# Three PSUM banks for the first image of a last layer, and another order of the SBUF pools of the layer before it

## The chip, the cores and the metric

The kernel runs on one core of a Trainium2 chip. The metric is the time of one execution on the device in microseconds (us), as the median of several runs. Everything the kernel computes, all four layers for all four images, lies in one launch.

## The reference, cut to what matters

Four images of 64 x 64 points with 128 channels pass through four layers. Each layer normalises its input over groups of four channels (`_gn`), does its own work, and adds the result to the input:

```python
x = x + _L0_conv_ref(_gn(x), ...)   # selective scan in four directions
x = x + _L1_conv_ref(_gn(x), ...)   # Fourier mixing along rows and columns, two dense layers
x = x + _L2_conv_ref(_gn(x), ...)   # attention between channels, spectral convolutions
x = x + _L3_conv_ref(_gn(x), ...)   # attention of each point to its 7 x 7 neighbours
```

The last layer, cut to its core, is this (4 heads of 32 channels, `SCALE = 32 ** -0.5`):

```python
qkv = x @ qkv_w.T + qkv_b                 # q, k, v for all points
kp, vp = pad(k, 3), pad(v, 3)             # zeros around the image
k_win, v_win = 7 x 7 windows of kp, vp
attn = softmax(einsum(q, k_win) * SCALE + bias)
out = einsum(attn, v_win) @ proj_w.T + proj_b
```

All arithmetic is in fp32.

## The kernel before, in words

The four layers run one after the other, each for all four images. The first two functions, `layer0` and `layer1`, are not touched. `layer1` (Fourier mixing) works image by image. Its last instructions for each eighth of an image are the second dense matrix (`po`, L686), a normalisation on VectorE, the addition to the input (L705) and the store to the buffer x2 in device memory (L706).

`layer2` (the third layer) takes the images in pairs. `layer2_image` is a generator that builds one image's instructions in steps. `Pace.in_turn` interleaves the generators of two images by a rough clock of its own, and `manual_schedule` keeps that order on TensorE, ScalarE, VectorE and GpSimd. The profile shows nearly all of this layer as L872, so one goes by the names of tiles. An image's input is the tile `xg`, loaded in four quarters. Its last steps scale and add up `m`, `sp` and `z`, and store `m` to the buffer x3 in four quarters. The layer makes its SBUF pools in one line: `l2big` with seven arrays of 16 KB per partition, `l2tmp` with work tiles, and `l2small` with columns.

`layer3` (the last layer) first makes a pool of weights and of padded key images, `l3w`. It loads six weight arrays (L1412), clears a tile `zero` on VectorE (L1418), clears the edges of the key images `kp` on GpSimd (L1421), and clears the edges of two padded value images `v_pads` in device memory by eight transfers from `zero` (L1423, L1425). Then it makes its working pools and, under `manual_schedule`, does the following:

- `front(b)` loads image b (`x3`, in four quarters) and then has four parts. The norm: for each of eight chunks of 512 points, four transposes into a PSUM tile `pg` (L1443), `bn_stats` on VectorE (L1444), and a copy to `xn` on ScalarE (L1445). The scale and offset of the groups (L67 to L79) and their application (L1451). The values: for each chunk four products into a PSUM tile `pv` (L1456), the bias added into an SBUF tile `vt` on VectorE (L1464), and two stores to `v_pads` (L1467). The keys: for each chunk one product into a PSUM tile `pk` (L1471), and an ScalarE instruction that puts it into `kp` (L1474).
- `queries(b, by)` computes the queries of a row of eight blocks (`pq`, L1485, `q`, L1489) and loads the 16 value windows `V` of that row (L1500).
- The loop runs over 128 units of two blocks each, as a software pipeline: scores `ps` (L1561), bias and maximum (L1572, L1579), exponentials (L1552), the division on GpSimd (L1545), transposes `pt` (L1507), the product with the values `po` (L1595).

For image 0, `front(0)` and `queries(0, 0)` run in full before the loop. For images 1 to 3 the pieces of `front` are dealt out one by one between the units of the image before.

In PSUM the layer has three kinds of pools that matter here. `psM` has one bank, and `pg`, `gn_gm`, `gn_gv`, `pv`, `pk`, `pq` and `pj` all share it through one tag. `psS` has two buffers of two banks for the scores `ps`. `psT` and `psO` hold the transposes and the products with the values. Before the loop starts, `psS` is not in use.

All stores and loads named above are issued by SyncE, whose queue is executed in order: a transfer that has to wait holds up those behind it. SyncE's place for each transfer is set by the scheduler when the program is built.

SBUF pools are laid out in order of creation. A pool that is made after others have been closed may get their bytes. In the built program the first instructions on such a pool wait for the last users of every closed pool whose bytes it overlaps, whichever of the pool's tiles they touch. In the kernel before, the bytes of each partition are these:

| pool | bytes |
|---|---|
| layer1: `l1big` (input images and others) | from 32096 |
| layer2: `l2big` | 32096 to 146784 |
| layer2: `l2tmp`, `l2small` | 146784 to 228224 |
| layer3: `l3w` (weights, `kp`, `zero`) | 32096 to 77568 |
| layer3: `l3big` (`x3`, `xn`) | 77568 to 143104 |

So `l2big` takes bytes of `l1big`, and `l3w` takes bytes of `l2big`.

Of the kernel before, what the change touches and what calls it, by code (L numbers as in the profile page):

```python
# [2 lines left out]

# [7 lines left out]
F32 = mybir.dt.float32  # L11
# [5 lines left out]
P = 128  # L17
# [5 lines left out]
CH = 512  # L23
# [685 lines left out]
def load_image(nc, x, x_dram):  # L709
    for q in range(4):  # L710
        nc.sync.dma_start(
            x[:, 8 * q : 8 * q + 8, :], x_dram[1024 * q : 1024 * q + 1024, :].rearrange("(j p) d -> p j d", p=P)
        )
# [652 lines left out]
def layer2(sh, w, wp, x_in, x_out, scr, wt):  # L1366
    tc, nc = sh.tc, sh.nc
    with ExitStack() as ctx:
        pool = lambda name, bufs, **kw: ctx.enter_context(tc.tile_pool(name=name, bufs=bufs, **kw))
        ps = pool("l2ps", 3, space=PSUM)  # L1370
        for name, shape in (("XG", [64, 5, P]), ("BD", [P, P])):
            w[name] = [wp.tile(shape, F32, name=f"{name}{n}") for n in range(2)]
            for t in w[name]:
                nc.vector.memset(t, 0.0)
        for t in w["XG"]:
            nc.vector.memset(t[:, 4, 64:65], 1.0)
        pools = pool("l2big", 1), pool("l2tmp", 1), pool("l2small", 1), ps
        paced = copy(sh)
        paced.nc = Pace(nc)
        engines = {mybir.EngineType.PE, mybir.EngineType.Activation, mybir.EngineType.DVE, mybir.EngineType.Pool}  # L1380
        free = [0, 1]
        pairs = [[] for _ in range(NB // 2)]

        def image(b):
            n = free.pop(0)
            yield from layer2_image(paced, w, pools, x_in(b), x_out(b), (scr(n), scr(2 + n)), wt, n, pairs[b // 2])
            free.append(n)

        with tc.manual_schedule(engines=engines):
            paced.nc.in_turn((image(b) for b in range(NB)), 2)  # L1390


def layer3(sh, A, x_in, out, v_pads):
# [5 lines left out]
    with ExitStack() as ctx:  # L1399
        pool = lambda name, bufs, **kw: ctx.enter_context(tc.tile_pool(name=name, bufs=bufs, **kw))  # L1400
# [25 lines left out]
        big, tmp, small = pool("l3big", 2), pool("l3tmp", 2), pool("l3small", 4)  # L1426
        psS, psT = pool("l3psS", 2, space=PSUM), pool("l3psT", 2, space=PSUM)
        psO, psM = pool("l3psO", 1, space=PSUM), pool("l3psM", 1, space=PSUM)
# [2 lines left out]

        def front(b):

            x = big.tile([P, NJ, DM], F32, name="x3")
            load_image(nc, x, x_in(b))
            xn = big.tile([P, NT], F32, name="xn3")
            image[b] = x, xn
            yield
            st = small.tile([P, NCH, 6], F32, name="gn_st", bufs=2)
            for c in range(NCH):  # L1440
                pg = psM.tile([P, CH], F32, name="pg3", tag="m")
                for q in range(4):
                    nc.tensor.transpose(pg[:, q * P : (q + 1) * P], x[:, 4 * c + q, :], sh.ident)  # L1443
                nc.vector.bn_stats(st[:, c, :], pg)  # L1444
                nc.scalar.copy(xn[:, c * CH : (c + 1) * CH], pg)  # L1445
                yield
            s_, o_ = sh.group_scale(st, psM, small, "m")
            yield
            for c in range(0, NT, NT // 2):
                xc = xn[:, c : c + NT // 2]  # L1450
                nc.vector.tensor_scalar(xc, xc, s_, o_, ALU.mult, ALU.add)  # L1451
            yield
            for c in range(NCH):
                pv = psM.tile([P, 4, P], F32, name="pv3", tag="m")
                for q in range(4):
                    nc.tensor.matmul(  # L1456
                        pv[:, q, :],
                        lhsT=xn[:, (4 * c + q) * P : (4 * c + q + 1) * P],
                        rhs=w["qkv"][:, 2 * P : 3 * P],
                        start=True,  # L1460
                        stop=True,
                    )
                vt = tmp.tile([P, 4, P], F32, name="vt")
                tt(vt, pv, w["v_b"].unsqueeze(1).to_broadcast([P, 4, P]), ALU.add)  # L1464
                rows = v_pads[b % 2][3 + 8 * c : 11 + 8 * c, 3:67, :].rearrange("(q r) c d -> r c q d", r=2)
                for r in range(2):
                    nc.sync.dma_start(rows[r], vt[64 * r : 64 * r + 64])  # L1467
                yield
            for c in range(NCH):
                pk = psM.tile([P, CH], F32, name="pk3", tag="m")  # L1470
                nc.tensor.matmul(  # L1471
                    pk, lhsT=w["qkv"][:, P : 2 * P], rhs=xn[:, c * CH : (c + 1) * CH], start=True, stop=True
                )
                nc.scalar.activation(  # L1474
                    kps[b % 2][:, 3 + 8 * c : 11 + 8 * c, 3:67],
                    pk.rearrange("p (h w) -> p h w", w=64),
                    AF.Identity,
                    bias=w["qkv_b"][:, 1:2],
                )
                yield  # L1480
# [49 lines left out]
        with tc.manual_schedule(engines=engines):  # L1530
            for _ in front(0):
                pass
            rows = {0: queries(0, 0)}
            for s in range(NU + 6):
                b, p = divmod(s, 32)
# [18 lines left out]
                if s < NU:  # L1554
                    q, V = rows[s // 4]
                    ps = psS.tile([P, 2, CH], F32, name="ps3")
# [52 lines left out]
                if p == 7 and b + 1 < NB and s < NU:  # L1609
                    pieces = front(b + 1)  # L1610
# [12 lines left out]
def network(tc, A, out):  # L1623
    nc = tc.nc
    with ExitStack() as ctx:
        const = ctx.enter_context(tc.tile_pool(name="const", bufs=1))
        dram = ctx.enter_context(tc.tile_pool(name="dram", bufs=1, space=bass.MemoryType.DRAM))
        sh = Shared(tc, const, A)
        x1, x2, x3 = ([dram.tile([NT, DM], F32, name=f"x{n}_{b}") for b in range(NB)] for n in (1, 2, 3))
        scr = [dram.tile([NT, DM], F32, name=f"scr{n}") for n in range(4)]  # L1630
        wt = dram.tile([32, 2, 8 * Q], F32, name="wt2")
        l0 = {n: dram.tile([NT, 2 * P], F32, name=f"l0_{n}") for n in ("y0", "y1", "y20", "y21", "y3")}
        l0 |= {n: dram.tile([2, P, NT], F32, name=f"l0_{n}") for n in ("xr0", "xr1", "xw0", "xw1", "z0", "z1", "z2")}
        l0 |= {f"W{n}": dram.tile([4, WD], F32, name=f"l0_W{n}") for n in ("00", "01", "10", "11")}
        l0 |= {f"B{n}": dram.tile([NS, CH], F32, name=f"l0_B{n}") for n in range(3)}
        layer0(sh, A, lambda b: A["x"][b], lambda b: x1[b], l0.__getitem__)
        l2w = ctx.enter_context(tc.tile_pool(name="l2w", bufs=1))
        w2 = layer1(sh, A, lambda b: x1[b], lambda b: x2[b], l2w, wt)
        layer2(sh, w2, l2w, lambda b: x2[b], lambda b: x3[b], lambda n: scr[n], wt)
        v_pads = [dram.tile([70, 70, DM], F32, name=f"l3_v{n}") for n in range(2)]  # L1640
        layer3(sh, A, lambda b: x3[b], lambda b: out[b], v_pads)
# [182 lines left out]
```

## Time and profile before

| | |
|---|---|
| median of 3 runs | 8356.34 us (8350.67 to 8357.69) |
| span of the profiled execution | 8355.5 us |
| busy: TensorE, VectorE, ScalarE, GpSimd | 79%, 81%, 76%, 66% |

The answer of the trace for four stretches of time, one for each layer, gives this (busy us of each engine, and the share of full speed that TensorE's clock was granted):

| layer | stretch, us | length | TensorE | VectorE | ScalarE | clock |
|---|---|---|---|---|---|---|
| 0 | 0 to 6071 | 6071.0 | 4802.08 | 5452.26 | 5453.76 | 0.97 |
| 1 | 6071 to 6690 | 619.0 | 518.34 | 307.94 | 152.92 | 0.91 |
| 2 | 6690 to 7743 | 1053.0 | 761.45 | 564.87 | 340.35 | 0.81 |
| 3 | 7743 to 8355.5 | 612.5 | 510.23 | 431.58 | 386.01 | 0.90 |

How to read it: the shares of the whole span are those of layer 0, which takes nearly three quarters of the time and is not touched. What the change concerns lies in the joints between the layers 1, 2 and 3, and in the first 85 us of the last layer. There the chain of waits has to be read piece by piece in order of time. Its rows give a start, a length, and the engine with the tile and line, or `SPq` for the issue of a transfer by SyncE, or `DMA` for a transfer's way from issue to landing.

### The profile page before, as it was taken

Reading aid. Unit: us, or ns where it says so; the run is one execution under the profiler, and the core shown is the slowest. Engines: PE = TensorE matmul, PEld = TensorE weight load, DVE = VectorE, ACT = ScalarE, POOL = GpSimd, SP = SyncE. Lnnn points to the kernel's source line nnn. Section 1 sums busy time; section 2 is a strip of 40 time slices with the busy share of each in tenths; the row PEclk is TensorE's granted clock in tenths of the full one; section 3 lists DMA queues with packets and bytes.
Section 4 is the critical chain, followed back from the end, with each engine's and each line's share of the span. In section 5 each row is a group of like instructions: output and inputs, shape, how many; then the busy total and the mean of one; then the engine's idle time right before and its main releaser. Section 6 shows DMA issues by size and latency. Waiting matters only on the chain.

```text
span 8355.5 us, 140584 instructions
## 1 busy us (share of the span) xinstructions
PE 6592.1 (79%) x52976; PEld 4182.2 (50%) x52976; DVE 6756.6 (81%) x7952; ACT 6333.0 (76%) x10320; POOL 5485.2 (66%) x2502
## 2 busy tenths in 40 slices
PE   7588888778788777888887777787778978686689
PEld 3344454444445444444544444454457756464456
DVE  2689999998899999889999999999944545645578
ACT  6799999999899889989989999999822213315467
POOL 0689889988888889888888999999800011020233
PEclk9799999999999999999999999999989988788799
DMA  6445555444555554455555445554432041331332
GB/s 111 132 144 179 166 170 173 164 160 156 169 169 177 175 171 153 154 176 159 175 173 175 163 153 181 177 175 169 165 94 52 18 118 38 86 100 31 95 93 78
DMA packets 1281978, 1163.79 MB, mean 139 GB/s; under 512 B 637973, under 2 KB 1075825, under 8 KB 1214354
## 3 DMA queue, kind: packets, MB, share of 16 engines
q1 hardware_dynamic: 1279618, 1153.06, 43.6%
q8 instruction: 417, 6.83, 0.3%
q14 instruction: 263, 2.15, 0.1%
q10 hardware_dynamic: 1680, 1.74, 0.1%
HBM read 962.66 MB, written 189.74 MB: 138 GB/s over the span
## 4 chain that ended last, share of the span: by engine, by line
PE 21%; ACT 11%; DVE 10%; issue 3%; POOL 2%; DMA 2%; SPq 1%; ACTq 0%; DVEq 0%; POOLq 0%
DVE h L484 4%; ACT hT L381 4%; ACT dA L483 4%; PE pt L371 2%; POOL dB L477 1%; PE po L686 1%; PE pf L681 1%; PE pz L872 1%; PE pt L1507 1%; PE pu L872 1%; DVE in_st L872 1%; PE pb L872 1%; PE ps L1561 1%; DVE m L872 1%; PE pa L872 1%
## 5 line engine op out<-in xcount | busy, mean ns | idle before, releaser
L484 DVE TENSOR_TENSOR_SCAN h<-dA,state,dB 128x512 f32<-128x512 f32 x4096 | 4962.0, 1270 | 379.5 <-ACT dA L483 269.8
L477 POOL TENSOR_TENSOR dB<-du,Bb 128x1024 f32<-128x1024 f32 x2048 | 4820.0, 2385 | 567.4 <-DVE h L484 398.0
L371 PE MATMUL pt<-ident,h 128*128 128x128 f32 x16384 | 2256.9, 282 | 1023.1 <-ACT hT L381 1018.9
L371 PEld LDWEIGHTS pt<-ident,h 128*128 128x128 f32 x16384 | 1846.3, 143 | 2063.8 <-ACT hT L381 1815.1
L483 ACT ACTIVATE dA<-delta,A_neg 128x512 f32<-128x512 f32 x4096 | 2745.6, 690 | 157.8 <-DVE h L484 136.7
L381 ACT COPY hT<-pt 128x1024 f32<-128x1024 f32 x2048 | 2068.9, 1010 | 182.5 <-PE pt L371 169.3
L406 PE MATMUL yT<-hT,W 128*32 128x256 f32 x16384 | 1400.9, 415 | 2.7 <-DVE y L422 2.1
L872 POOL COPY XG<-Xs 64x9 f32<-64x9 f32 (+2 forms) x44 | 11.0, 294 | 1024.9 <-ACT Xs L872 1024.9
L406 PEld LDWEIGHTS yT<-hT,W 128*32 128x32 f32 x16384 | 454.3, 150 | 353.6 <-issue 338.4
L206 PE MATMUL cv<-xn,taps 128*128 128x512 f32 x1152 | 620.1, 639 | 8.7 <-DVE e L222 8.7
L1545 POOL TENSOR_TENSOR S<-S,sm 128x784 f32<-128x784 f32 x128 | 191.4, 1495 | 408.2 <-DVE sm L1543 347.3
L317 PE MATMUL dp<-xd,w_dt 65*128 65x512 f32 x512 | 300.0, 669 | 105.4 <-ACT Ct L304 92.0
L326 POOL TENSOR_TENSOR du<-delta,u 128x1024 f32<-128x1024 f32 x128 | 305.1, 2384 | 78.5 <-DVE delta L323 78.5
L206 PEld LDWEIGHTS cv<-xn,taps 128*128 128x128 f32 x1152 | 185.5, 190 | 248.5 <-issue 244.6
L298 PE MATMUL xd_ps<-u,w_x 128*48 128x512 f32 x512 | 251.1, 614 | 44.0 <-DMA u<-l_xw 19.8
L1552 ACT ACTIVATE S<-S,mx 128x196 f32<-128x196 f32 x512 | 227.9, 448 | 32.7 <-DVE mx L1579 32.2
L682 ACT ACTIVATE h<-pf,b 128x512 f32<-128x512 f32 x128 | 88.0, 687 | 145.0 <-PE pf L681 145.0
L323 DVE SCALAR_TENSOR_TENSOR delta<-delta,dp 128x512 f32<-128x512 f32 x256 | 169.3, 661 | 27.7 <-ACT delta L321 27.7
L317 PEld LDWEIGHTS dp<-xd,w_dt 65*128 65x128 f32 x512 | 79.4, 195 | 220.7 <-ACT Ct L304 150.6
L1421 POOL MEMSET kp<- 128x210 f32 (+1 forms) x8 | 1.8, 287 | 275.0 <-DMA x<-m 275.0
L320 ACT ACTIVATE delta<-dp 128x512 f32<-128x512 f32 x256 | 152.4, 595 | 30.1 <-PE dp L317 25.6
L1507 PE MATMUL pt<-ident,S 128*98 128x128 f32 x1024 | 165.2, 285 | 4.4 <-POOL S L1545 1.9
(336 smaller groups left out, 7282.4 us busy)
## 6 DMA issues: line engine op xcount, KB each, us to landing
Bb<-l_B SPq DMA_DIRECT2D x512, 1024.0 KB
W<-l_W SPq DMA_DIRECT2D x512, 256.0 KB
l_y<-y SPq DMA_DIRECT2D x128, 512.0 KB
u<-l_xw SPq DMA_DIRECT2D x64, 512.0 KB
y<-l_y SPq DMA_DIRECT2D x64, 512.0 KB
u<-l_xr SPq DMA_DIRECT2D x64, 512.0 KB
V<-l_v SPq DMA_DIRECT2D x512, 49.0 KB
wr<-wt SPq DMA_DIRECT2D x128, 136.0 KB
```

What stands on the lines that cost most here:

```text
L206: nc.tensor.matmul(pm, lhsT=taps[:, s, t, :], rhs=xn[:, dy : dy + 8, dx : dx + 64], start=(t == 0), stop=(t == 8),)
L298: nc.tensor.matmul(xd_ps, lhsT=w_x[:, s, k, :], rhs=u[:, s, :], start=(s == 0), stop=(s == 1))
L317: nc.tensor.matmul(dp, lhsT=w_dt[:, k, s * P : (s + 1) * P], rhs=xd, start=True, stop=True)
L326: nc.gpsimd.tensor_tensor(du, delta, u, ALU.mult)
L371: nc.tensor.transpose(pt[:, j, s, :], G["h"][:, s, t0 : t0 + 32, :].rearrange("p t n -> p (t n)"), sh.ident)
L381: return lambda: nc.scalar.copy(hT, pt.rearrange("p j s d -> p j (s d)"))
L406: nc.tensor.matmul(U["yT"][e][32 * jo : 32 * jo + 32, qo % 2, :], lhsT=U["Ws"][G["g"]][:, :, 4 * q + j], rhs=hT[:, j, :], start=((e, jo) n ...
L477: nc.gpsimd.tensor_tensor(dB, du, B_now[:, q : q + 1, :].to_broadcast([P, 2, CH]), ALU.mult)
L483: nc.scalar.activation(dA, delta[:, s, :], AF.Exp, scale=A_neg[:, k, s, n : n + 1])
L484: nc.vector.tensor_tensor_scan(h[:, s, :, q], dA, dB[:, s, :], state[:, s, n : n + 1], ALU.mult, ALU.add)
L872: r = f(*args, **kw)
L1507: nc.tensor.transpose(pt[:, half, hp, :], U["S"][:, e, hp, 98 * half : 98 * half + 98], sh.ident)
```

## The change

The change has two parts. In `front`, a counter gives the PSUM tiles of image 0 in turn to three banks: one of three goes to `psM` as before, and two of three take the first half of a buffer of `psS`. For the images 1 to 3, and for `gn_gm`, `gn_gv`, `pq` and `pj`, nothing changes. In `layer2` the pools are made in another order, with `l2big` last.

```diff
@@ layer2
-        pools = pool("l2big", 1), pool("l2tmp", 1), pool("l2small", 1), ps
+        tmp, small, big = pool("l2tmp", 1), pool("l2small", 1), pool("l2big", 1)
+        pools = big, tmp, small, ps
@@ layer3, front
+            ring = itertools.count()
+
+            def bank(name):
+                if b == 0 and next(ring) % 3:
+                    return psS.tile([P, 2, CH], F32, name="ps3")[:, 0, :]
+                return psM.tile([P, CH], F32, name=name, tag="m")
+
...
-                pg = psM.tile([P, CH], F32, name="pg3", tag="m")
+                pg = bank("pg3")
...
-                pv = psM.tile([P, 4, P], F32, name="pv3", tag="m")
+                pv = bank("pv3").rearrange("p (q d) -> p q d", q=4)
...
-                pk = psM.tile([P, CH], F32, name="pk3", tag="m")
+                pk = bank("pk3")
```

The first part is meant to let TensorE fill one bank while VectorE and ScalarE empty another. The second part moves the bytes: `l2tmp` then lies at 32096 to 99424, `l2small` behind it, and `l2big` at 113536 to 228224. The pool of weights of the last layer, at 32096 to 77568 as before, then overlaps `l2tmp` and no longer `l2big`, and `l2big` no longer overlaps `l1big`.

On TensorE, ScalarE, VectorE and GpSimd the order of the instructions of the layers stays as it was, but for the clearing of `zero` and the scaling of the query bias on VectorE and the clearing of edges on GpSimd, which now stand in the tail of the third layer. On SyncE the transfers move as follows. The eight loads of `xg` for the first pair of images stand directly behind the last store of layer 1, ahead of all `wr` loads; four of those stood ahead of them before. The 14 transfers of weights and zeros (L1412, L1423, L1425) stand in the tail of the third layer, before the stores of its last images, where they wait for the last products `pb` of that layer. The loads of `x3` follow directly on the last store of the third layer.

More of the change, by code (lines that the diff above doesn't have):

```diff
@@ L1 @@
+import itertools
 from contextlib import ExitStack
```

## The prediction

> **What bounds the kernel now.** I read the table of stretches first, to see which layers have slack, and then the chain of waits in order of time at the two joints and in the first part of the last layer. There it runs through every instruction of image 0, one behind the other. Columns: start, length, what.
>
> ```profile
> 6690.04 2.98 DMA x<-x
> 6693.02 0.02 SPq L872
> 6693.04 0.03 issue
> 6693.07 4.46 DMA xg<-x
> 6697.53 0.45 issue
> 6697.98 3.66 PE pg L872 x16
> ```
>
> The third layer's input is loaded only when layer 1's last store has landed. The same happens at the next joint, with 14 issues of SyncE after the landing (shown in part):
>
> ```profile
> 7739.86 3.17 DMA x<-m
> 7743.11 0.35 SPq L1412
> ...
> 7749.98 0.61 SPq L1425
> 7750.59 0.04 issue
> 7750.63 4.42 DMA x<-x
> ...
> 7755.29 1.10 PE pg L1443 x4
> 7756.48 0.71 DVE gn_st L1444
> 7757.26 0.59 ACT xn L1445
> 7757.86 0.04 issue
> 7757.90 1.13 PE pg L1443 x4
> ...
> 7782.55 2.09 PE pv L1456 x8
> 7784.66 0.70 DVE vt L1464
> 7785.37 0.04 issue
> 7785.41 2.09 PE pv L1456 x8
> ```
>
> With one bank, chunk n+1 starts when chunk n has been emptied: 2.6 us a chunk in the norm, 2.86 us in values and keys. The table of stretches (length, busy us of TensorE, its weight loads, VectorE, ScalarE, GpSimd, then the clock) shows what this does to the clock:
>
> ```profile
> 6698.00:6702.00 4.00, 4.00 (x21) 3.97 (x22) 2.43 (x4) 0.00 (x0) 0.00 (x0) 0.55 1.16 291
> 6702.00:6704.20 2.20, 1.61 (x13) 1.17 (x11) 2.01 (x4) 0.00 (x0) 0.00 (x0) 1.00 1.17 290
> 7780.00:7828.00 48.00, 34.98 (x82) 18.46 (x81) 6.37 (x9) 6.00 (x9) 0.00 (x0) 0.50 0.30 82
> ```
>
> 73% busy keeps half clock for 48 us; dense transposes reach full clock within 4 us.
>
> **What the Trainium skill says.** "TensorE: Matmul & The Clock Gate", Part 1: the clock stands at half by default and is released after about 3.4 us of sustained work. The trace agrees: work starts at 6697.98 and the mean of 0.55 over 4 us puts the release near 6701.6, 3.6 us later. "PSUM — Partial Sum Buffer", PSUM bank collisions: two engines must not touch one bank at once, two reads included; so inside a chunk the copy on ScalarE stays behind `bn_stats`, as the rows at 7756.48 and 7757.26 show, and only other banks give overlap. "DMA: Bandwidth & Descriptors", Anatomy of one DMA: a fixed part of about 2 us, mostly until the last byte is confirmed. The trace has 2.42 us for a store of `vt` (chain, 7918.13), and that is what I use.
>
> **The change part by part.**
>
> *Joint of layers 1 and 2.* The last store is issued at 6690.04 and takes SyncE 0.50 us. The first load of `xg` now stands behind it in the queue and waits for products and ScalarE work done by 6686.5. So it is issued at 6690.6 instead of 6693.07: 2.5 us. I keep 4.46 us to landing. Bounds 2.0 (the store's bytes are still in the engines) and 3.0 (four `wr` loads no longer ahead). All later work of the layer hangs on this chain in the same order, so all shifts. The `wr` loads are needed 200 us later.
>
> *Joint of layers 2 and 3.* The load of `x3` overlaps bytes of the third layer and still waits for its last store, which lands at 7743.03. The 14 issues between (7743.11 to 7750.59) are gone from here: 7.5 us. Bounds 7.3 and 8.0, the latter if the load lands sooner with no zero stores in flight. What the 14 cost where they now stand: SyncE reaches them at 7674.4, when the last `pb` is done, needs some 7.5 us, and in the run before had nothing to issue from 7671.71 to 7689.33. Behind them wait the stores of `m` and the reloads of `sp`, first due at 7689.33. VectorE's clearing of `zero` (0.38 us) falls into a gap of 1.83 us before 7679.35, in which VectorE waits for `in_pm`. The scaling of the bias (0.15 us) waits for its load; with 1.75 us from issue to use as before, that is there by 7677, and VectorE reaches the place near 7682. GpSimd (1.81 us of clearing) idles there for 275 us. So 0 to 0.3 us; I take 0.
>
> *Norm of image 0.* From the first transposes to `gn_gm` it takes 7755.29 to 7775.57 = 20.3 us. With three banks a chunk can follow each 0.86 us at half clock (four transposes at 0.213). A bank comes back after 1.10 + 0.09 + 0.70 + 0.08 + 0.59 = 2.6 us, a third of which is 0.87. A quarter of the image (two chunks) lands each 1.5 us (512 KB at 346 GB/s). So the last chunk starts near 6.1 us, at full clock or nearly, and ends at 6.7; `bn_stats` and aggregation take it to 7.9, `gn_gm` to 8.3. Saved: 12.0 (11.5 to 12.5). The chain from `gn_gm` to the first `pv` (4.15 us) stays; in it TensorE does nearly nothing and falls back to half clock, as it did by 6708.3.
>
> *Values.* Before: 8 x 2.86 = 22.9 us. Now PSUM is no longer the limit, but `vt` has two tiles, so group c waits until the stores of group c-2 have landed. A store takes SyncE 0.61 (median), two 1.24; landing 2.42 later; between the pairs the queue has two loads of `V` at 0.73. From the first `pv` (0): `vt` 0 is done at 2.8 and 1 at 4.6 (TensorE, 1.78 a group at half clock). Stores of 0 land at 6.6, so `vt` 2 ends at 7.3; stores of 1 land at 8.4, so 3 ends at 9.1. SyncE then issues in order, with landings at 11.9 and 13.2 (`vt` 4 at 12.6, 5 at 13.9), 16.4 and 17.7 (6 at 17.1, 7 at 18.4). This is a wait the row of `vt` hardly shows before, 1.1 us in one instance (front of image 1).
>
> *Keys and queries.* Key group 0 needs the bank of `vt` 5, 1 that of 6, 2 that of 7. From group 1 (17.1) TensorE is dense: half clock, 1.75 a group, until about 20.8, then 0.9 (a key product took 1.06 at full clock in the loop, with its tail). Group 7 ends at 25.4, `pq` at 26.4, `q` at 27.1, the first `ps` at 27.3. Before, first `pv` to first `ps` was 7779.72 to 7828.40 = 48.7. Saved: 21.4. At half clock throughout, the first `ps` is at 32.1: 16.5.
>
> *The loop.* It then runs as before. The ten remaining `V` loads of the first row follow the last `vt` stores: near 19.7 + 10 x 0.73 = 27, while the first `po` comes 12.6 us after the first `ps`.
>
> Sum: 2.5 + 7.5 + 12.0 + 21.4 = 43.4. 8356.3 - 43.4 = 8313.
>
> **The rivals.**
>
> 1. *TensorE stays at half clock in values and keys.* For: it did so for 48 us at 73% busy, and stores of `vt` leave gaps again. Against: from key group 1 nothing interrupts it. 43.4 - 4.9 = 38.5: 8318.
> 2. *The `vt` stores don't bind.* For: one wait of 1.1 us was all in the loop. Against: there the groups come 3.5 us apart. Two groups at half clock, 14 at 0.9, `pq` and `q`: first `ps` at about 18.5, saved 30: 8304.
> 3. *The loop doesn't take the gain of the values and keys*, because the `V` loads, some 48 for three rows, now start later relative to the loop and hold it. Against: row 1 is needed some 25 us after the first `ps` and done 11 us after it. It would leave 22: 8334.
> 4. *Not faster.* The third layer is 1053 us long at a mean clock of 0.81, in which TensorE is busy 761. If its shift of 2.5 us against the windows of the clock lowered the grant to 0.77, TensorE would take some 5% longer; were all of that on the chain, some 45 us are lost: about 8358, slower than before. For: the clock there swings between 0.5 and 1. Against: order and gaps of the layer stay the same, so hits and misses should even out.
>
> **How the numbers follow.** Forecast 0.56, rival 1 0.20, rival 2 0.12, rival 3 0.07, rival 4 0.05. The range 8300 to 8330 holds the forecast and the first two rivals with the bounds of the joints (1 us) and of the run medians (the three runs before span 7 us), and leaves out rivals 3 and 4. Rivals 1 to 3 are all over 0.2% (17 us) faster: 0.95. Of rival 4 I give 0.03 to no difference and 0.02 to slower.
>
> **What would show it.** In the profile of the changed kernel: `xg` issued about 0.5 us after the last store of layer 1; no L1412 between the last `x<-m` and the load of `x3`; first `pg` to `gn_gm` in 8 to 9 us; `vt` released by DMA from its third group on; the clock at 1.0 in the last key groups; first `pv` to first `ps` in 27 us; the stretch from there to the end as long as before (527 us). The prediction is wrong if the third layer's stretch changes its length by over 5 us, if VectorE stalls near its tail for `qkv_b`, or if the loop waits for `V`.

## The result

| | before | after |
|---|---|---|
| median of 4 runs | 8353.5 us (8348.6 to 8357.7) | 8318.2 us (8312.7 to 8325.7) |
| span of the profiled execution | 8355.5 us | 8311.1 us |
| mean clock of TensorE | 0.942 | 0.948 |

After over before is 0.9959, with a 95% interval from 0.9941 to 0.9976: faster, by about 34 us. The forecast was 8313, with a range from 8300 to 8330. The two profiled executions differ by 44.4 us and the medians by 35.3; the runs of the changed kernel spread over 13 us. Its profiled execution is one of two short ones (8312.9 and 8312.7; the other two took 8323.6 and 8325.7), and that of the kernel before one of its longer ones (8356.3), so the profiles show more of a gain than the medians.

### The profile page after: what moved, and what is told of

It reads as the page before. It is cut to its first block, busy times and chain, and to the rows that moved or that the text cites. A ratio compares the mean times of both kernels' runs of the same rounds, so it can differ in the third digit from the quotient of the medians.

```text
span 8311.1 us, 140578 instructions
## 1 busy us (share of the span) xinstructions
PE 6570.4 (79%) x52976; PEld 4173.6 (50%) x52976; DVE 6756.3 (81%) x7952; ACT 6330.8 (76%) x10320; POOL 5482.4 (66%) x2502
## 4 chain that ended last, share of the span: by engine, by line
PE 21%; DVE 11%; ACT 10%; issue 3%; POOL 2%; DMA 2%; SPq 1%; ACTq 0%; DVEq 0%; POOLq 0%
DVE h L485 5%; ACT hT L382 4%; ACT dA L484 3%; PE pt L372 2%; POOL dB L478 1%; PE po L687 1%; PE pf L682 1%; PE pt L1516 1%; PE pz L873 1%; PE pu L873 1%; DVE in_st L873 1%; PE pb L873 1%; PE ps L1570 1%; PE pa L873 1%; DVE m L873 1%
## 5 line engine op out<-in xcount | busy, mean ns | idle before, releaser
L873 POOL COPY XG<-Xs 64x9 f32<-64x9 f32 (+2 forms) x44 | 10.9, 292 | 1027.8 <-ACT Xs L873 1027.8
L1561 ACT ACTIVATE S<-S,mx 128x196 f32<-128x196 f32 x512 | 227.9, 448 | 34.1 <-DVE mx L1588 33.5
L322 ACT ACTIVATE delta<-delta 128x512 f32<-128x512 f32 x256 | 162.4, 634 | 7.9
```

The costliest lines, as they stand in the source:

```text
L873: r = f(*args, **kw)
```

## The profile after

The chain of waits at the joint of layers 1 and 2 (start, length, what):

```profile
6689.73 0.36 SPq L707
...
6690.19 0.45 SPq L873
...
6692.40 7.35 DMA xg<-x
6699.75 0.14 issue
6699.88 0.64 PE pg L873 x4
```

The first `xg` load is issued 0.46 us after layer 1's last store, where it was 3.03 before. The wait for the store's landing is gone from the chain, and what holds the first norm now is the landing of the load's last quarter.

The chain at the joint of layers 2 and 3, and through the norm of image 0:

```profile
7740.31 3.17 DMA x<-m
7743.49 0.02 issue
...
7743.69 3.78 DMA x<-x
7747.47 0.24 issue
7747.71 1.09 PE pg L1452 x4
7748.80 1.71 PE ps L1452 x8
7750.51 0.94 PE pg L1452 x4
7751.45 0.87 PE ps L1452 x4
...
7755.14 0.38 DVE gn_mv L68
...
7755.66 0.37 PE gn_gm L70 x2
```

The 14 issues are gone from between the last store and the load of `x3`. From the last store's issue to the first `pg` it takes 7.40 us (15.43 before). The transposes follow one another through three banks (two of them bear the name `ps`), and `gn_gm` comes 7.95 us after the first `pg` (20.28 before).

The chain through the values:

```profile
7759.42 2.07 PE ps L1465 x8
7761.49 1.64 PE pv L1465 x8
...
7763.15 0.70 DVE vt L1473
...
7763.87 0.57 SPq L1476
...
7764.49 2.38 DMA l_v<-vt
...
7767.00 0.70 DVE vt L1473
```

The last row is the fourth `vt`: it waits until the second store of the second one, issued at 7764.49, has landed 2.38 us later (the third waits in the same way for the first). VectorE's waits in this stretch (us in total, times, longest) say it of all six groups from the third on:

```profile
DVE vt L1473 <- DMA l_v<-vt: 9.4, 6, 3.7
```

The table of stretches (columns as in the table before) shows what the clock does with these gaps:

```profile
7764.00:7768.00 4.00, 3.21 (x27) 2.83 (x26) 1.38 (x2) 0.00 (x0) 0.00 (x0) 1.00 0.47 120
7768.00:7772.00 4.00, 0.90 (x8) 0.71 (x7) 0.65 (x1) 0.00 (x0) 0.00 (x0) 1.00 0.57 147
7772.00:7776.00 4.00, 3.12 (x11) 1.55 (x11) 1.35 (x3) 0.69 (x1) 0.00 (x0) 0.64 0.57 149
7776.00:7780.00 4.00, 4.00 (x5) 1.67 (x6) 0.77 (x2) 1.00 (x2) 0.00 (x0) 0.50 0.53 138
7780.00:7784.00 4.00, 4.00 (x10) 1.71 (x9) 0.00 (x0) 3.12 (x5) 0.00 (x0) 1.00 0.28 77
```

TensorE reaches full clock, idles at the `vt` wait (0.90 us busy in 4), does the first keys at half clock, and the last at full clock. From the first `pv` to the first `ps` it takes 26.48 us (48.68 before).

**One link of this chain misleads.** Further on, the chain runs through SyncE's issues of `V` loads and then ends them like this:

```profile
7788.58 2.42 DMA V<-l_v
7791.00 0.03 issue
7791.03 1.50 POOL S L1554
```

That reads as if GpSimd's first division waited for a `V` load. But `S` is divided by `sm`, whose reciprocal on VectorE ran from 7790.77 to 7790.95. Experiment e3_vt8 tells which of the two it was.

## Where the first joint's gain went

The last `x<-m` is issued at 7740.31, and it was at 7739.86 before: although layer 2's first group scale (`gn_s`) comes 3.2 us earlier, the layer ends 0.45 us later. TensorE's products in the two traces, put side by side by their place in its order, are 2.2 to 4.0 us ahead until 7107, and 3.8 us there. There the chain of waits has this, before:

```profile
7111.34 1.99 PE pa L872 x8
7113.34 1.93 PE pb L872 x8
7115.26 1.09 PE pu L872 x8
```

and after:

```profile
7107.52 3.78 PE pa L873 x8
7111.31 3.46 PE pb L873 x8
7114.76 1.09 PE pu L873 x8
```

The same 16 products start 3.82 us earlier and end 0.50 us earlier: 1.79 + 1.53 = 3.32 us are lost in them. There is no wait between them. The stretch in which most of them run has the clock (the third number from the end) at 1.00 before and at 0.50 after:

```profile
7112.00:7116.00 4.00, 4.00 (x22) 2.35 (x21) 0.04 (x1) 2.10 (x5) 0.00 (x0) 1.00 0.00 0
```

```profile
7108.00:7112.00 4.00, 4.00 (x10) 2.57 (x11) 0.00 (x0) 1.61 (x3) 0.00 (x0) 0.50 0.00 0
```

The Trainium skill, "TensorE: Matmul & The Clock Gate", Part 1, says that the clock follows a free-running window of activity, so that the same kernel meets full clock at different instructions from run to run. That fits; what these runs show is only that the same products got another clock. This is the largest single change of the lead and not the only one: it grows again to 2.8 us near 7340, turns to 0.8 us behind at 7470, and ends 0.3 to 0.5 us behind.

## The experiments

The stages of all runs from their profiles, in us. "1>2": from layer 1's last store to layer 2's first `gn_s`. "2": from there to the last `in_d` of layer 2 that is made from `in_st`; TensorE's 5468 products in it are the same in all runs. "2>3": from that `in_d` to `gn_gm` of the last layer. "3": `gn_gm` to first `ps`. "Loop": from there to the end. The last columns give the median of the runs, and the ratio of the runs to those of the kernel before on the same chip, with its interval (it is not the quotient of the two medians); a single run has no interval.

| run | 1>2 | 2 | 2>3 | 3 | loop | median | ratio |
|---|---|---|---|---|---|---|---|
| before | 17.2 | 1013.7 | 54.7 | 52.8 | 527.1 | 8353.5 | |
| after | 14.3 | 1017.3 | 34.4 | 30.2 | 525.2 | 8318.2 | 0.9959 [0.9941, 0.9976] |
| e6_after | 14.5 | 1016.3 | 34.4 | 31.2 | 526.2 | 8312.9 | 0.9952 [0.9938, 0.9966] |
| e1_pools | 14.6 | 1018.0 | 47.0 | 52.8 | 524.0 | 8351.5 | 0.9989 [0.9981, 0.9997] |
| e2_banks | 17.6 | 1024.1 | 42.0 | 29.7 | 526.7 | 8327.5 | 0.9960 [0.9947, 0.9972] |
| e4_norm | 14.3 | 1014.8 | 34.1 | 52.3 | 528.0 | 8339.1 | one run |
| e5_two | 14.6 | 1019.2 | 37.3 | 29.6 | 523.9 | 8317.3 | 0.9953 [0.9941, 0.9966] |
| e3_vt8 | 15.0 | 1021.3 | 34.3 | 22.4 | 520.0 | 8309.2 | 0.9938 [0.9925, 0.9950] |
| e7_vt4 | 14.2 | 1013.4 | 34.5 | 22.8 | 518.6 | 8297.9 | one run |
| e11_onebank_vt8 | 17.5 | 1018.5 | 54.5 | 52.9 | 521.9 | 8361.0 | one run |
| e12_before | 17.1 | 1013.4 | 54.7 | 52.8 | 527.0 | 8358.5 | one run |
| e8_early | 14.5 | 1017.1 | 29.5 | 22.0 | 521.1 | 8298.2 | 0.9924 [0.9910, 0.9938] |
| e9_stats | 14.6 | 1016.5 | 23.8 | 21.9 | 517.3 | 8288.9 | 0.9921 [0.9907, 0.9934] |
| e10_warm | 14.6 | 1020.4 | 23.9 | 19.7 | 521.9 | 8289.1 | 0.9923 [0.9911, 0.9936] |

Columns 2>3 and 3 move only when something in them is changed, and else repeat to 1.6 us. Column 2 moves by up to 10.7 us between kernels that do the same work there. The kernel before measured 8363.5 beside e1, e2, e3 and e8, 8359.0 beside e5, e6, e9 and e10, and 8362.4 (one run) beside the four single runs; so ratios are to be compared, not medians.

**e1_pools: the order of the pools alone.**

```diff
-        pools = pool("l2big", 1), pool("l2tmp", 1), pool("l2small", 1), ps
+        tmp, small, big = pool("l2tmp", 1), pool("l2small", 1), pool("l2big", 1)
+        pools = big, tmp, small, ps
```

> The order of the pools alone, one bank as before. My theory: the two joints are shorter by 2.9 us (xg loads right behind the last store) and 8.0 us (from the last store's issue to the first pg 7.4 us where it was 15.4), and the first 85 us of the last layer stay: first pg to gn_gm 20.3, first pv to first ps 48.7. So 8353.5 - 8.0 - 2.9 = 8342.6, if layer 2 keeps what its joint gives it. Rival, the clock: what a joint ahead of layer 2 gives or takes is lost or doubled inside the layer by where half-clock stretches of TensorE fall, so that only the 8.0 is sure: 8339 to 8349. Rival, no effect of the pools (the 14 issues cost as much in the tail as they did at the joint): 8353.

Measured: joint 1>2 shorter by 2.6 us, 2>3 by 7.7 (54.7 to 47.0), the rest of the front unchanged. The median is 8351.5 beside 8363.5. The theory's stages hold, and the rival of no effect falls. That of the clock stays open: column 2 is 4.3 us longer in this profile than in that of the kernel before. The 14 transfers cost nothing in the tail: from the last `in_d` to the last store it takes 19.01 us in this run, in before and in after.

**e2_banks: the three banks alone**, with the old line for the pools.

> The three banks alone, pools in the old order. My theory: the parts are independent, so first pg to gn_gm is 8.0 us (20.3 before), first pv to first ps 26.5 (48.7 before), the joints stay as before (15.4 us from the last store's issue to the first pg): 8353.5 - 12.3 - 22.2 = 8319, or 8317 if the loop is again 2 us shorter. Rival: the two parts need each other (the zero stores, still in flight beside the first vt stores, make these later): first pv to first ps 29 or more, 8322 or above.

2>3 is shorter by 12.7 us, 3 by 23.1, and the first `pv` to the first `ps` takes 26.1 us: the parts are independent, and the rival falls by its stage. The time of 8319 was missed (8327.5), but it was worked out from 8353.5; beside 8363.5 the gain is 36 us where 34.5 were expected. The stages that it shares with the kernel before (columns 1>2 and 2) are together 10.8 us longer, which hides a third of the gain in this profile. The ratio of the runs (0.9960) equals that of the whole change: its interval, 10 us to each side, doesn't resolve the pools' part there.

**e4_norm: three banks for the norm, one for values and keys.**

```diff
-                pv = bank("pv3").rearrange("p (q d) -> p q d", q=4)
+                pv = psM.tile([P, 4, P], F32, name="pv3", tag="m")
...
-                pk = bank("pk3")
+                pk = psM.tile([P, CH], F32, name="pk3", tag="m")
```

> The change with three banks for the norm alone, values and keys on one bank as before. My theory: the parts of the sum are separate: first pg to gn_gm 7.9 us as in the change, gn_gm to the first ps 52.8 as before, so 22.6 us longer than the change from the last store to the end. Rival, the stretches share a cause (the clock: a norm at full clock leaves TensorE faster in the values): gn_gm to first ps under 50.

First `pg` to `gn_gm` takes 7.7 us, `gn_gm` to the first `ps` 52.3: as the theory said, and the rival (under 50) falls. From the last store to the end it is 595.4 us, 24.6 more than the first profile of the change and 22.6 more than the second.

**e5_two: psM every second time.**

```diff
-                if b == 0 and next(ring) % 3:
+                if b == 0 and next(ring) % 2:
```

> Every second PSUM tile of image 0 on psM instead of every third, so psM comes round after two chunks. My theory: a bank's round of 2.6 us sets the norm's pitch, 1.3 us a chunk with two and 0.87 with three: first pg to gn_gm 11.4 us (7.9 in the change); values and keys are held by the landings of the vt stores and keep their 30.2 us from gn_gm to the first ps: 3.5 us longer than the change in all. Rival, two banks are enough (VectorE or the load sets the pitch of the norm): no difference to the change. Rival, PSUM also holds values and keys: gn_gm to first ps 33 or more.

First `pg` to `gn_gm` is 10.9 us (7.9 in the change), 3 stays at 29.6. The bank's round sets the pitch of the norm, as the chain shows: two chunks for each round of `pg`, `gn_st`, `xn`, 2.53 us apart:

```profile
7753.81 1.13 PE pg L1452 x4
...
7754.97 0.71 DVE gn_st L1453
...
7755.70 0.59 ACT xn L1454
...
7756.34 1.13 PE pg L1452 x4
```

The third bank is worth 2.9 us in the norm, and nothing in values and keys.

**e3_vt8 and e7_vt4: more tiles for `vt`** (eight, as shown, and four).

```diff
-                vt = tmp.tile([P, 4, P], F32, name="vt")
+                vt = tmp.tile([P, 4, P], F32, name="vt", bufs=8)
```

> The change with eight vt tiles instead of two. My theory (the landings of the vt stores hold values and keys): no vt waits for a DMA; two groups at half clock, the others at 0.9 to 1.0, first pv to first ps near 18.5 us (26.5 in the change), the rest as long as before: 8318 - 8 = 8310, loop unchanged because the first row's V loads end near 25 us after the first pv and the first po comes at 30. Rival: TensorE's half clock holds the stretch, first pv to first ps 24 or more: 8316. Rival: issues of SyncE hold the start of the loop, as the chain of the changed kernel says (SPq, then V): then the first po stays where it was, some 38.7 us after the first pv, and the time is 8318.

> The change with four vt tiles. My theory, from the landings of the run with eight (the pair of stores of group k lands near 6.1 + 1.55 k us after the first pv): only group 7 still waits, by 0.5 us: gn_gm to first ps 22.9 (22.4 with eight, 30.2 with two). Rival: a wait for one landing holds the next stores too, and it runs away as with two tiles: 26 or more.

With eight tiles 3 takes 22.4 us and with four 22.8 (two: 30.2 and 31.2), and the first `pv` to the first `ps` 18.8 us with eight (18.5 expected). VectorE's waits for `vt` name only TensorE with eight:

```profile
DVE vt L1473 <- PE ps L1465: 2.8, 5, 1.0
DVE vt L1473 <- PE pv L1465: 1.4, 3, 1.0
```

With four there is a rest, in three groups rather than the one expected, and most of it costs nothing:

```profile
DVE vt L1473 <- DMA l_v<-vt: 2.7, 3, 2.0
```

So the landings of the `vt` stores were the bound, as the prediction had it, and two of its rivals fall: the clock alone doesn't hold the stretch, and the stores do bind. The chain's hint at SyncE falls too. With eight tiles no `V` load is issued before 7781.24 (in the change the first stood at 7765.35, between the stores), yet the loop starts 1 us earlier, and the chain enters it without SyncE:

```profile
7784.81 0.94 PE ps L1570 x16
...
7789.70 0.19 DVE sm L1552
7789.89 0.07 issue
7789.95 1.50 POOL S L1554
```

First `ps` to first `pt` is 6.69 us in both runs, although in this one the sixteenth `V` load is issued near 7793 (24 issues took 19.30 us from 7781.24 on), after that division has ended. GpSimd's wait is for `sm`; the `V` landing in the chain of the changed kernel was a coincidence of 0.05 us.

More `vt` tiles also shorten the loop, which was expected unchanged. The values of images 1 to 3 are made in its first three quarters: from the maximum (`mx`) of the first unit to that of the 97th it takes 411.7 to 415.7 us in the eight runs with two tiles, and 405.7 to 410.3 in the six with four or eight. How the tiles do this isn't shown: in the loop of the changed kernel VectorE waits for a landing of `vt` once, for 1.4 us.

**e11_onebank_vt8: the kernel before, with eight `vt` tiles.**

> The kernel before, with eight vt tiles. My theory: with one bank a group takes 2.86 us, longer than two tiles need, so nothing is gained in the first image: gn_gm to first ps 52.8 as before; in the loop, where the values of images 1 to 3 wait for landings here and there, some 4.5 us are gained as in the other runs with eight tiles: 8349. Rival: vt was a limit beside the bank already: gn_gm to first ps 50 or less.

3 stays at 52.9, and the loop is 5.1 us shorter. So bank and `vt` limit one behind the other: only when the banks are there do the tiles matter in the first image. The time of 8349 was missed (8361.0): column 2 was 4.8 us longer than in the first profile of before, which took back the loop's gain, and the two layers ahead of it were together 4.0 us longer (layer 1 some 7 longer, layer 0 some 3 shorter).

**e6_after: the changed kernel again; e12_before: the kernel before again.**

> The changed kernel itself again, as the measure for its neighbours. My theory: the last layer repeats to 1 us (last store to gn_gm 15.3, gn_gm to first ps 30.2), while the layers before it, whose instructions are the same, differ by up to 10 us from the profile of the first run, because the grant of TensorE's clock falls on other instructions each time. Rival, the layers before repeat as well, and the spread between runs has its place in the last layer, at the vt stores: then gn_gm to first ps differs by several us.

> The kernel before again, for the length of layer 2, whose instructions are the same in all runs with the old order of the pools. My theory: from the last store of layer 1 to the last store of layer 2 took 1049.8 us in the first profile and 1060.6 in that of the three banks alone; a third value will fall anywhere between 1047 and 1062, by where TensorE runs at half clock. Rival: the three banks, or the chip, made the 1060.6: 1049 to 1051.

Of e6 the last layer repeats to 2.0 us (1 was expected), and the layers before it came within 2.0 us as well, so its profile decides between neither theory. Its five runs reach from 8308.0 to 8322.6, a spread like that of the first four (8312.7 to 8325.7). e12 came out at 1049.5 us from store to store, inside the rival's range, so it decides nothing by itself; but e11, whose layer 2 is the same work without the three banks, took 1055.0 on the same chip. Banks and chip are thereby not needed for a difference of 5 us.

Over all 14 profiles column 2 goes from 1013.4 to 1024.1. But the two pairs of profiles of one kernel lie close: 1013.7 and 1013.4 before, 1017.3 and 1016.3 after. So no two runs of one kernel show the 10 us; they lie between kernels, and on several chips. In the layers ahead, where all kernels issue the same products, one kernel does differ from itself: from before to e12 the way to layer 1's first `pu` is 5.6 us shorter and the way from there to its last store 7.3 us longer. Whether chance, the chip or something fixed in each kernel sets column 2 stays open.

**e8_early, e9_stats, e10_warm: beyond the change.** The load of `x3` for image 0 waits for bytes only; its data have been in memory since the second pair of images began. e8 (with eight `vt` tiles) therefore places `l3big` first, on the bytes of `l2tmp`, with a small pool for `zero` and the query bias behind it, and `l3w` after these:

```diff
+        big, zp = pool("l3big", 2), pool("l3z", 1)
+        first = big.tile([P, NJ, DM], F32, name="x3")
+        load_image(nc, first, x_in(0))
...
         wp = pool("l3w", 1)
```

> Eight vt tiles, and the pool of the last layer's images placed first, on the bytes of the third layer's work tiles, with zero and the query bias behind it; the weights then wait for the third layer's end. My theory (the load of x3 waits for the bytes, not for its data, which have been in memory since the second image pair began): x3 is loaded near 7683, in the tail of the third layer, the first pg stands ready before the last store, and the norm begins when VectorE is done with the third layer, near the issue of the last store: some 7 us less between it and gn_gm plus 1 to 2 us of overlap of the norm's start, so 8310 - 8.5 = 8301.5. The five weight loads (some 3 us of issue after the last store has landed) are there before the first pv. Rival: the weights or the key edges, which now wait for the third layer's last store, take the place of x3: then the first pv comes no earlier than about 7743.5 + 5 + 2.4 and some 3 us are gained: 8307. Rival: loads and zero stores in the tail hold up the last stores of m: joint as before, 8310.

`x3` is loaded from 7671.08 on, 66 us ahead of the last store, and its first three chunks are transposed 13 us before it. But 2>3 falls by 4.8 us against e3, not by 8.5; the medians, 8309.2 and 8298.2, differ by 11.0, so the time alone would have passed for a confirmation. VectorE's timeline (start, length, engine, line, operation; in brackets the idle time before, and what ended it) has the reason:

```profile
7740.05 0.70 DVE L1458 BATCH_NORM_STATS2 gn_st<-pg 128x6 f32<-128x512 f32 x1 [3.39 <-DMA x<-m]
```

The first `bn_stats` waits for the last store's landing, by a rival that I hadn't named: not the weights, but the tile of the statistics, whose pool lies on the stored tile's bytes. e9 gives that tile another place:

```diff
+        st0 = zp.tile([P, NCH, 6], F32, name="gn_st0")
...
-            st = small.tile([P, NCH, 6], F32, name="gn_st", bufs=2)
+            st = small.tile([P, NCH, 6], F32, name="gn_st", bufs=2) if b else st0
```

> The version with the early load of x3, with the statistics of image 0 (gn_st) also on bytes of the third layer's work tiles. There the first bn_stats began 3.37 us after the last store's issue, at its landing. My theory: that wait was for the bytes of gn_st, which lie on those of the last stored tile; now bn_stats follows VectorE's last m directly: last store to gn_gm 7.1 us instead of 10.45, so 3.4 us less. Rival: the copies to xn, or something else that waits for the landing (the weights' pool), take its place: 10.4 as before.

2>3 falls by another 5.7 us to 23.8; 3.4 were expected. VectorE's order has changed with it: `bn_stats` now stands between the last instructions of layer 2, ahead of the store:

```profile
7735.48 1.23 DVE L873 TENSOR_TENSOR m<-m,sp 128x1024 f32<-128x1024 f32 x1
7736.62 0.69 DVE L1459 BATCH_NORM_STATS2 gn_st<-pg 128x6 f32<-128x512 f32 x1
7737.23 1.21 DVE L873 TENSOR_TENSOR m<-m,z 128x1024 f32<-128x1024 f32 x1
7738.36 1.29 DVE L1459 BATCH_NORM_STATS2 gn_st<-ps 128x6 f32<-128x512 f32 x2
```

The last store is 1.0 us later by this, and `gn_gm` follows its issue by 3.7 us (7.1 expected, 15.3 in the change). At 0.9921 against 0.9952 beside it, e9 is the shortest version: 8288.9 us, 24 less than the change on the same chip.

e10 adds to e9 six groups of transposes into idle banks, around the group statistics; the results aren't read:

```diff
+            warm(2)
             s_, o_ = sh.group_scale(st, psM, small, "m")
+            warm(4)
```

> The same with six groups of four transposes into the idle banks of psT around the group statistics, whose results nobody reads: two before gn_gm, four after gn_gv; nothing else is changed. My theory: TensorE falls to half clock because it idles for 4 us between the last pg and the first pv; kept at work, it begins the values at full clock, and two to three groups take 0.9 us instead of 1.7 to 2.1: gn_gm to first ps 22.0 before, 19.5 here. Rival: the transposes don't fill the wait well enough (VectorE's steps between leave 1 us gaps), or a part of them ends after xn is ready: gn_gm to first ps 22 or more.

3 falls from 21.9 to 19.7 us, as expected. The stretch in which the values begin, at 7746.23 in e9 and at 7748.74 in e10, behind the last of the added transposes:

```profile
7746.00:7750.00 4.00, 3.77 (x17) 3.77 (x18) 2.12 (x3) 0.00 (x0) 0.00 (x0) 0.50 0.02 4
```

```profile
7746.00:7750.00 4.00, 3.43 (x29) 3.19 (x30) 3.11 (x6) 0.26 (x1) 0.36 (x2) 1.00 0.49 129
```

The first eight products of the values take 2.08 us in e9 and 1.16 in e10. But the reason that was expected is not right: in e9 the idle chain doesn't drop the clock, which is at 0.50 ahead of it already, as it is in e10:

```profile
7738.00:7742.00 4.00, 2.22 (x8) 1.42 (x8) 3.21 (x6) 2.15 (x4) 0.16 (x1) 0.50 0.45 131
```

```profile
7738.00:7742.00 4.00, 3.43 (x15) 2.63 (x13) 3.96 (x6) 1.18 (x3) 0.00 (x0) 0.50 0.43 129
```

The added transposes bring the clock up before the values begin. In the whole time it doesn't show (0.9923 beside 0.9921): column 2 and the loop of its profile are 8.5 us longer than e9's.

## Why the prediction was right

By its steps, with what the first profile of after has for each:

| step | forecast | measured |
|---|---|---|
| joint of layers 1 and 2 | 2.5 | 2.9 at `gn_s`; -0.8 (a loss) at the last store of layer 2 |
| joint of layers 2 and 3 | 7.5 | 8.0 |
| the 14 transfers in the tail | 0 to 0.3 | 0 |
| norm of image 0 | 12.0 | 12.3 |
| `gn_gm` to first `pv` | 0 | 0.4 |
| values, keys, queries | 21.4 | 22.2 |
| loop | 0 | 1.9 |

- **First joint.** The size was right at its place; the sentence that all later work shifts with it was not. In these two profiles it shifts as far as the first products that get another clock. Rival 4 named this mechanism and bounded it at 45 us (its 5% of the 761 us of TensorE is nearer 40); column 2 differs by 10.7 us over 14 profiles. Whether some of the 2.9 us remains on average can't be told from this spread: with the new order column 2 has 1013.4 to 1021.3, with the old one 1013.4 to 1024.1, and the mean is 1017.4 in both. The sign of a wrong prediction, a change of layer 2 by over 5 us, is thereby within what the layer differs by without the change: from before to e2, 10.4 us.
- **Second joint.** The upper bound came true, as was said with it, because the first quarter of `x3` landed sooner, in 3.78 us rather than 4.42. From its issue to the first `pg` it takes 4.0 to 4.3 us in all runs that load it there with the new order and 4.5 to 4.7 in those with the old one; that it is the zero stores that were in the way isn't shown by itself.
- **Norm.** Right in size and cause; e5 shows the cause, the round of a bank.
- **Values and keys.** Right in cause: the landings of `vt` hold six groups, and e3, e7 and e11 show that they, not the bank, were what remained. From the first `pv`, the last `vt` ends at 18.0 us (forecast 18.4), TensorE reaches full clock in the keys near 20.6 (20.8), and the first `ps` comes at 26.5 (27.3). Not foreseen was the full clock in between, from 7764 to 7772.
- **Loop.** Unchanged within its spread: from the first `ps` to the end, the runs with two `vt` tiles have 523.9 to 528.0 us.
- **The sum** of 43.4 us compares with 44.4 in the two profiles and 46.1 between the medians of e6 and its before; the first medians had 35.3. That it comes so near the profiles is in part luck: instead of the 2.5 us of the first joint there are -0.8 at the end of layer 2, and the loop's 1.9 us and small gains in the other steps make up for them. The median of 8318.2 is just the time of rival 1, so the time alone could not have told that rival from the forecast; the profile does.

Rival 1 (half clock throughout values and keys) and rival 2 (no `vt` wait) are both refuted by the rows above; rival 3 (the loop waits for `V`) by the time from first `ps` to first `po`, 12.24 us (12.62 before), and by the loop, which is no longer than before.

## What to carry to other kernels

When a single PSUM bank is the limit, ask what becomes the limit with three: here it was the number of SBUF tiles whose stores must land, and four tiles instead of two gave 7 us more in the first image and some 6 in the loop. A transfer at a joint of two stages may wait for bytes and not for data, and every small tile that lies on bytes still being stored can make the same wait; so place first what the next stage needs first. A gain ahead of a long stretch with a swinging TensorE clock should be checked at the stretch's start and at its end, and against how far that stretch differs between runs of one kernel and between kernels that do the same work in it.

## What the runs showed of the hardware

- Layer 2, with the same products in the same order, took from 1013.4 to 1024.1 us in 14 profiles of 12 kernels; what sets it is open. Between before and after, 3.3 us of that lay in 16 products of 7 us that ran at half clock in one trace and at full clock in the other.
- In the changed kernel TensorE kept full clock in a stretch of 4 us in which it was busy 0.90 us (7768 to 7772), and had 0.64 and 0.50 in the next two, in which it was busy for 78% and 100%. With eight `vt` tiles, where it doesn't idle there, the clock stays at 1.00 in all four stretches from 7774 to 7790.
- Six groups of transposes of no use, put around the group statistics, brought the clock from 0.50 to 1.00 before the values began and made the way to the first `ps` 2.2 us shorter.
